# A graph layer on one core: the add of a block's products goes to the head of step 8, and words are unpacked five steps ahead of the turn of their keys

## The chip, the cores and the metric

One core of a Trainium2 chip. The metric is the device time of one launch in microseconds (us), the median of several runs. The profile is of one execution of the same program.

## The reference

One graph layer on 6250 nodes of 64 features and 206,250 edges, sorted by their target node:

```
h   = relu(layernorm(x))
msg = h[src] + edge_feat                  # 206250 x 64
agg = segment_sum(msg, dst, 6250)
out = x + relu(agg @ W1 + b1) @ W2 + b2   # 64 -> 128 -> 64
```

## The kernel before, in words

The sum over edges is split in two. The sum of `h[src]` is made as a product: for each group of three target nodes (a "tile" of at most 127 edges) the kernel counts how often each of the 6272 padded source rows occurs, as a matmul of two one-hot matrices, and multiplies the counts with `h`. The sum of the edge features is made by matmuls of the features with one-hot matrices of the target nodes.

**Blocks and steps.** The work is cut into 23 blocks of 84 tiles (252 nodes), each block into 14 steps of 6 tiles. One loop over all steps `n` writes out the order of instructions on every engine by hand (the scheduler takes them as written); `b` is the block and `s` (0 to 13) the step within it. Each engine takes its own instructions in this order, and waits at an instruction until what it needs is there. The parts of a step, in the order in which the loop calls them:

- `tops` and `before`: lists of small jobs that are hung on single steps (copies of turned keys, unpacking, the checks "over" of L897, the adds of a bias `add_b2`, L1049).
- `count(n)`, on odd steps: 12 matmuls `pc<-hotb` (L962) on TensorE; ScalarE then copies the counts to a ring in SBUF (`ring<-pc`, L971).
- `rows_of_tiles`, on every third step: two VectorE instructions that make `hotb` (L949), the one-hot rows of 18 tiles (three steps), about three steps ahead of the counts that read them.
- `encode`, on every sixth step (n % 6 == 2): three VectorE instructions (L932 twice, L938) that prepare the rows of 36 tiles.
- `products(b - 1, ...)`, at steps 1, 3, 5 and 7: 12, 12, 12 and 13 matmuls `pv<-ring,h` (L981) for the block before.
- `add_products(b - 1)`, at step 8: VectorE adds that block's finished products from PSUM to the sums in SBUF (L1016, in the first four blocks the copy L1014). The block is then `ready`.
- `mlp`, at step 10 (and at step 5 for a few blocks that come late): `ph<-sums,w1s` (L1059) of the ready block on TensorE, relu on ScalarE (L1061); some steps later the second product (`po`, L1067), its add to `x` on VectorE (L1073) and the store.
- `later` and `turns`: jobs that earlier steps have hung on this one. Among them are the sums of edge features. A block has three units of two chunks; VectorE makes a unit's one-hot matrix `hotf` (L496) at steps 3, 6 and 10, and TensorE multiplies it with the features into `bank` (L509) at step 9 (first unit, 48 matmuls) and step 11 (second and third unit, 96 matmuls). `hotf` has two buffers.

`ph`, `po`, `pw`, `pcols` and `over` share one PSUM buffer, one after the other.

**Words and keys.** The positions of a tile's edges come as packed words, 128 tiles at a time and two such lists in one fetch: an indirect DMA `words<-packed` on POOL's queue, which is otherwise full of gathers `pfeat<-table` (rows of `h` for the last 17 groups of edges, eight gathers for a group, summed by L572). `unpack` decodes two lists in four parts on VectorE, one part a step: the fields (L725 to L728), the offsets (L732, L735), the check (L738, L739) and the digits (L743 to L749). At step `n`, the turn of the keys, TensorE transposes them (`pk`, L762). The planner looks for the last step early enough, and prefers step 13 of a block:

```
TURNS = (13, 8, 3)
...
n = min((n for n in range(deadline(c0) + 1 - TURN[-1][0]) if n % STEPS in (TURNS if i > 2 else (4 * i - 2,)) and c1 - R <= encoded(n)),
        key=lambda n: (i > 2 and TURNS.index(n % STEPS), -n))
```

For the pairs i = 4, 6, 8, 10, 12 and 14 this gives step 13 of blocks 4, 7, 10, 13, 16 and 19 (the last pair has one list only). The unpacking begins `ahead` steps before that, and the fetch of the words is put at the head of POOL's list 16 steps before the unpacking. Which gathers POOL gets in a step is decided by an estimated clock and by gates at steps 9 and 11, so the fetch's place moves the gathers around it.

Of the kernel before, what the change touches and what calls it, by code (L numbers as in the profile page):

```python
# [68 lines left out]
SB = 3  # L69
# [3 lines left out]
FRESH = 8  # L73
# [78 lines left out]
def gnn_kernel(ctx: ExitStack, tc: tile.TileContext, x, src_t, dst_t, dst_g, edge, w1, b1, w2, b2, out):  # L152
# [10 lines left out]
    def nodes(b):  # L163
        return start[b + 1] - start[b]
# [4 lines left out]
    def block_of(n):  # L169
        b = min(n // STEPS, NW - 1)  # L170
        return b, n - b * STEPS
# [360 lines left out]
    def at_columns(b, a, z):  # L532
        return [(u, v, c - ring_from(b)) for u, v, c in ring_runs(b, a, z)]
# [174 lines left out]
    def fetch_pair(i0):  # L708
        n = min(2, IC - i0)
        fetch_words(i0, n, P, [first_i[:, i:i + 1] for i in range(i0, i0 + n)])  # L710
# [91 lines left out]
    def unpack_pair(i0):  # L802
        n = min(2, IC - i0)
        return unpack(i0, n, P, nfirst[:, i0:i0 + n], min(P, NWIN - i0 * P) if n == 1 else P)
# [3 lines left out]
    def columns(i):  # L808
        a, z = i * P, min(i * P + P, NWIN)
        mid = min(max(SX, a), z)  # L810
        return [(u - a, v - a, u + o) for u, v, o in ((a, mid, 0), (mid, z, NX)) if u < v]
# [115 lines left out]
    def encode(k):  # L927
        c, n = k * EB % R, min(EB, TILES - k * EB)
        at = work.tile([P, EB, 2, A8], BF16, name="at", bufs=1)
        of = work.tile([P, EB, 2, WE], BF16, name="of", bufs=1)  # L930
        for to, iota_k, m, key in ((at, iota_a, A8, kq[:, 0]), (of, iota_w, WE, kq[:, 1])):
            nc.vector.tensor_tensor(  # L932
                to[:, :n].rearrange("s i k (m o) -> s (i k) m o", o=2),
                iota_k.rearrange("s (m o) -> s m o", o=2).unsqueeze(1).to_broadcast([P, 2 * n, m // 2, 2]),
                key[:, c:c + n].rearrange("s i k o -> s (i k) o").unsqueeze(2).to_broadcast([P, 2 * n, m // 2, 2]),
                op=OP.is_equal)
        pairs_of = of[:, :n].rearrange("s i k (m o) -> s (i k) m o", o=2)
        nc.vector.tensor_tensor(pairs_of, pairs_of, kv[:, c:c + n].rearrange("s i k o -> s (i k) o").unsqueeze(2)  # L938
                                .to_broadcast([P, 2 * n, WE // 2, 2]), op=OP.mult)
        codes[k] = at, of  # L940

    def rows_of_tiles(j):
        if j * HT >= TILES or j in hots:
            return
        at, of = codes[j * HT // EB]
        o, n = j * HT % EB, min(HT, TILES - j * HT)
        hot = hotb[:, j % HOTS]
        for k, c, m in ((0, 0, WS), (1, WS * A8, WL)):
            nc.vector.tensor_tensor(  # L949
                hot[:SLOTS, :n, c:c + m * A8].rearrange("s i (w a) -> s i w a", a=A8),  # L950
                at[:SLOTS, o:o + n, k].unsqueeze(2).to_broadcast([SLOTS, n, m, A8]),
                of[:SLOTS, o:o + n, k, :m].unsqueeze(3).to_broadcast([SLOTS, n, m, A8]), op=OP.mult)
        hots[j] = hot.bitcast(F8)

    def count(n):

        t0 = (n - 1) * ST
        m = min(PAIR, TILES - t0)
        pc = ps.tile([P, 1024], F32, tag="pc", name="pc")
        for j in range(m):  # L960
            hot = hots[(t0 + j) // HT][:, (t0 + j) % HT]
            nc.tensor.matmul(pc[:, j * WPC:j * WPC + HI], hot[:, :P], hot[:, P:P + HI], start=True, stop=True)  # L962
        b, s = block_of(n - 1)
        own = HI - (BY_VECTOR if n == NSTEP - 1 else 0)
        of = pc.bitcast(U8).rearrange("p (m h k) -> p h m k", h=WPC, k=4)
        for u, v, c in ring_runs(b, s * SC, s * SC + m * V):
            to = ring[:, :, c:c + v - u].rearrange("p h (m k) -> p h m k", k=V)
            u, v = u // V - s * ST, v // V - s * ST
            ends = (0, FIRST, own) if b < NW - 1 and s == STEPS - 2 else (0, own)
            for h, z in zip(ends, ends[1:]):  # L970
                nc.scalar.activation(to[:, h:z], of[:, h:z, u:v, :V], AF.Copy)  # L971
            if own < HI:
                nc.vector.tensor_copy(to[:, own:], of[:, own:HI, u:v, :V])

    def products(b, a, z):

        if a == 0:
            pvs[b] = ps.tile([P, 512], F32, tag="pv", name="pv")[:, :columns_of_block(b)]
        c = ring_from(b)
        for h in range(a, z):  # L980
            nc.tensor.matmul(pvs[b], h2[:, h, :], ring[:, h, c:c + columns_of_block(b)], start=(h == 0), stop=(h == HI - 1))  # L981
# [26 lines left out]
    def add_products(b):  # L1008
        pv = pvs.pop(b)
        n = nodes(b)  # L1010
        for a, z, c in at_columns(b, 0, n):
            to = agg[:, start[b] + a:start[b] + z]
            if b <= SB:
                nc.vector.tensor_copy(to, pv[:, c:c + z - a])  # L1014
            else:
                nc.vector.tensor_tensor(to, to, pv[:, c:c + z - a], op=OP.add)  # L1016
        if b == SB:
            for a, z, c in at_columns(b, n, n + NX * V):
                nc.vector.tensor_copy(tail[:, a - n:z - n], pv[:, c:c + z - a])
# [187 lines left out]
    def deadline(c):  # L1207

        return c // EB * EB // ST - EB // ST + AHEAD - 1
# [4 lines left out]
    def encoded(n):  # L1214

        return ((n - AHEAD) * ST // EB + 2) * EB

    def unpack_later(n, f):
        fs = []
        before.setdefault(n, []).append(lambda: fs.extend(f()))  # L1220
        for k in range(4):
            before.setdefault(n + k, []).append(lambda k=k: fs[k]())

    def turn_later(n, i, p, cols):
        for k, f in TURN:
            (turns if f in "kv" else tops).setdefault(n + k, []).append(
                {"k": lambda: turn_keys(i, p), "v": lambda: turn_values(i, p), "0": lambda: key_copies(i, 0, cols),
                 "1": lambda: key_copies(i, 1, cols), "p": lambda: value_powers(i, cols)}[f])

    for i in range(1, IC):  # L1230
        c0, c1 = columns(i)[0][2], columns(i)[-1][2] + columns(i)[-1][1] - columns(i)[-1][0]
        n = min((n for n in range(deadline(c0) + 1 - TURN[-1][0]) if n % STEPS in (TURNS if i > 2 else (4 * i - 2,)) and c1 - R <= encoded(n)),
                key=lambda n: (i > 2 and TURNS.index(n % STEPS), -n))
        if i > 1 and i % 2 == 0:
            ahead = 9 if i > 2 else 4
            before.setdefault(max(n - 16 - ahead, 3), []).append(lambda i=i: i > 2 and queue.insert(
                0, (WORDS_US * 2, lambda: fetch_pair(i))))
            unpack_later(n - ahead, lambda i=i: unpack_pair(i))
        assert n <= (NW - 1) * STEPS + 7
        turn_later(n, i, P, columns(i))  # L1240
# [11 lines left out]
    def clock(n):  # L1252

        return n * HEAD_US if n < STEPS else STEPS * HEAD_US + (n - STEPS) * STEP_US
# [6 lines left out]
    ready = []  # L1261
# [35 lines left out]
    assert len(PART) == FRESH + 1  # L1297
    for n in range(NSTEP):
        b, s = block_of(n)
        for f in tops.get(n, []) + before.get(n, []):  # L1300
            f()
        if n % 2:
            count(n)
        if n % (HT // ST) == 0:
            rows_of_tiles(n // (HT // ST) + 1)
        if n % (EB // ST) == AHEAD and n // (EB // ST) * EB + EB < TILES:
            encode(n // (EB // ST) + 1)
        if b and 1 <= s < FRESH:
            products(b - 1, PART[s], PART[s + 1])
        if b and s == FRESH:  # L1310
            add_products(b - 1)
            if b - 1 > SB:
                ready.append(b - 1)
        if n in SECONDS:
            k = SECONDS.index(n)
            add_seconds(2 * k)
            if 2 * k + 2 >= NX:
                ready[:0] = range(SB + 1)
        if s in LAYERS and ready:
            mlp(ready.pop(0), n, LAYERS[s])  # L1320
        for f in later.pop(n, []) + turns.pop(n, []):
            f()
        pair_ends(n)
        if n >= 3:
            if s in (GROUPS if b < NW - 1 else LAST_GROUPS) and h_next < G and fetched.get(h_next, 1e9) + LAND_US <= clock(n + 2):
                group_hot(h_next)
                at_step(n + 2, features_h, h_next)
                h_next += 1
                add_later(n + 5)
            if n == 3:  # L1330
                pool[0] = clock(n - 1) + OPENING_US
            pool_until(clock(n) + LAND_US)
# [5 lines left out]
    b = NW - 1  # L1338
# [148 lines left out]
```

## Time and profile before

| | |
|---|---|
| median of 3 runs | 392.6 us (389.06 to 393.69) |
| the profiled execution | 391.7 us |
| its span, first to last instruction | 390.0 us |
| mean granted TensorE clock | 0.987 |
| busy: TensorE, VectorE, ScalarE, POOL | 85%, 80%, 84%, 69% |

A row of the timeline gives the start in us, the time taken, the engine (PE is TensorE, DVE VectorE, ACT ScalarE, POOL GpSimd), the line, the instruction with output and inputs, how many are merged (x), and in brackets how long the engine stood idle before it and what ended that. A row of the waits gives who waited for whom: us in total, times, longest.

### The profile page before, as it was taken

What the parts mean: (1) busy time and instruction counts of PE and PEld (TensorE: products, weight loads), DVE (VectorE), ACT (ScalarE), POOL (GpSimd) and SP (SyncE); (2) the same over time, 40 slices, a digit from 0 to 9 for tenths busy, and PEclk for the clock granted to TensorE, in tenths of its full rate; (3) what the DMA queues carried; (4) which work ended last, traced back from release to release, by engine and by line L of the source; (5) the groups of instructions that cost most, each with busy time, mean ns of one, the idle gap of its engine ahead of it and who ended that gap; (6) DMA issues with size and microseconds to landing.
All of it is one profiled execution on the core that took longest, in us unless ns stands there. A gap on an engine that the chain in (4) does not pass through costs nothing.

```text
span 390.0 us, 17219 instructions
## 1 busy us (share of the span) xinstructions
PE 329.7 (85%) x7297; PEld 304.7 (78%) x7298; DVE 312.2 (80%) x814; ACT 326.3 (84%) x376; POOL 270.2 (69%) x206
## 2 busy tenths in 40 slices
PE   2043289989799989889989999899999999999983
PEld 1033278879789979878889999799989989998872
DVE  5758999999988968959799869977998789789320
ACT  6466679999879869989899999999989899999710
POOL 8574588888867867587777788678877787788100
PEclk9999999999989999999999999999999999999988
DMA  7935896969848869759579789868977986798300
GB/s 158 281 100 194 302 306 157 242 145 258 229 102 204 237 165 231 215 117 309 144 207 264 182 206 256 227 165 219 269 195 185 258 246 154 167 279 206 75 15 20
DMA packets 111954, 76.93 MB, mean 197 GB/s; under 512 B 30853, under 2 KB 107773, under 8 KB 111871
## 3 DMA queue, kind: packets, MB, share of 16 engines
q1 hardware_dynamic: 89076, 66.71, 56.8%
q0 software_dynamic: 20560, 8.28, 16.1%
q8 instruction: 59, 0.97, 1.1%
q10 hardware_dynamic: 2235, 0.79, 0.8%
q14 instruction: 24, 0.20, 0.1%
HBM read 71.49 MB, written 4.26 MB: 194 GB/s over the span
## 4 chain that ended last, share of the span: by engine, by line
PE 56%; DVE 9%; ACT 2%; DMA 2%; issue 1%; DVEq 0%; ACTq 0%
PE pv L981 26%; PE pc L962 9%; PE bank L509 8%; PE ph L1059 3%; DVE hotb L949 3%; PE po L1067 2%; PE pv L541 2%; PE bank L572 2%; DMA dstq<-in_dst_g,cols_i 2%; ACT ring L971 1%; PE pk L762 1%; DVE hotf L496 1%; DVE sums L1016 1%; PE pw L769 1%; ACT after L1061 1%
## 5 line engine op out<-in xcount | busy, mean ns | idle before, releaser
L971 ACT ACTIVATE ring<-pc 128x1764 fp32r<-128x1764 uint8 (+2 forms) x183 | 262.3, 1488 | 16.4 <-PE pc L962 13.5
L352 POOL DMA_INDIRECT pfeat<-table,src_p x132 | 222.7, 1687 | 70.3 <-PE bank L509 34.7
L981 PE MATMUL pv<-ring,h 128*128 128x252 f32 x1127 | 156.6, 289 | 1.4 <-ACT ring L971 1.0
L981 PEld LDWEIGHTS pv<-ring,h 128*128 128x128 f32 x1127 | 139.4, 191 | 2.5 <-ACT ring L971 2.0
L949 DVE TENSOR_TENSOR hotb<-at,of 127x576 int32<-127x576 bf16 x216 | 120.5, 600 | 1.6 <-DVE of L938 0.5
L962 PE MATMUL pc<-hotb 128*128 128x49 fp8e5 x1932 | 78.5, 186 | 1.5 <-ACT ring L971 0.7
L962 PEld LDWEIGHTS <-hotb 128*128 128x128 fp8e5 x1932 | 68.0, 98 | 10.8 <-issue 2.2
L509 PE MATMUL bank<-feat,hotf 128*18 128x64 f32 x3288 | 57.6, 222 | 2.2 <-DVE hotf L496 1.2
L509 PEld LDWEIGHTS bank<-feat,hotf 128*18 128x18 f32 x3288 | 48.4, 99 | 5.0 <-DVE hotf L496 1.5
L496 DVE TENSOR_TENSOR hotf<-rel,iota 128x432 f32<-128x432 bf16 x69 | 41.2, 597 | 1.4 <-PE bank L509 1.2
L1016 DVE TENSOR_TENSOR sums<-sums,pv 128x252 f32<-128x252 f32 (+2 forms) x28 | 8.5, 330 | 30.0 <-PE pv L981 30.0
L932 DVE TENSOR_TENSOR at<-iota_a,kq 128x576 bf16<-128x576 bf16 (+1 forms) x54 | 24.4, 451 | 0.2
L352 POOL DMA_INDIRECT words<-packed,first_i x15 | 18.6, 1238 | 7.4 <-issue 4.3
L1059 PE MATMUL ph<-sums,w1s 128*128 128x252 f32 (+2 forms) x50 | 17.1, 425 | 6.8 <-DVE sums L1016 3.9
L1061 ACT ACTIVATE after<-ph,b1s 128x252 f32<-128x252 f32 (+2 forms) x25 | 11.8, 473 | 12.4 <-PE ph L1059 12.4
L938 DVE TENSOR_TENSOR of<-of,kv 128x288 bf16<-128x288 bf16 (+1 forms) x54 | 16.8, 311 | 2.9 <-DVE of L932 0.5
L302 PE MATMUL psrc<-shift,src 128*64 128x128 f32 (+1 forms) x16 | 4.1, 435 | 17.7 <-ACT src L299 17.7
L352 POOL DMA_INDIRECT sums<-in_dst_g,row_i x15 | 15.7, 1048 | 4.6 <-issue 3.7
L782 ACT ACTIVATE kq<-pk 128x512 bf16<-128x512 f32 (+18 forms) x48 | 18.0, 465 | 0.2 <-PE pk L762 0.2
L302 PEld LDWEIGHTS psrc<-shift,src 128*64 128x64 f32 (+1 forms) x16 | 3.1, 244 | 17.7 <-ACT src L299 13.0
L932 DVE TENSOR_TENSOR of<-iota_w,kq 128x288 bf16<-128x288 bf16 (+1 forms) x54 | 16.4, 304 | 0.0
L1067 PE MATMUL po<-w2s,after 128*126 128x64 f32 (+2 forms) x100 | 15.8, 280 | 0.6 <-ACT after L1061 0.6
(187 smaller groups left out, 307.6 us busy)
## 6 DMA issues: line engine op xcount, KB each, us to landing
feat<-in_edge SPq DMA_DIRECT2D x137, 384.0 KB
pfeat<-in_edge SPq DMA_DIRECT2D x16, 256.0 KB
pfeat<-table,src_p POOLq DMA_INDIRECT x132
out_y<-after SPq DMA_DIRECT2D x23, 63.0 KB
xl<-in_x SPq DMA_DIRECT2D x2, 512.0 KB
table<-xl SPq DMA_DIRECT2D x2, 512.0 KB
after<-in_x SPq DMA_DIRECT2D x4, 252.0 KB
table<-xl SPq DMA_DIRECT2D x1, 544.0 KB
```

Of the source, the lines that this page charges most:

```text
L352: ins = nc.gpsimd.indirect_dma_start(out=rows, out_offset=None, in_=source, in_offset=bass.IndirectOffsetOnAxis(ap=index, axis=0), compute ...
L496: nc.vector.tensor_tensor(hot_of[u][:, :n].rearrange("p c j w -> p (c j) w"), rel[:, c:c + n].rearrange("p c q k -> p (c q k)").unsqueeze( ...
L509: ins = nc.tensor.matmul(bank[q * QP:q * QP + WQ, at:at + D], hot_of[u][:, c, j, :], feats[u][c][:, j, :], start=(k == 0), stop=(k == JP - 1))
L782: nc.scalar.activation(kq[:, q, at:at + n].rearrange("s i k o -> s (i k) o"), pk[:, q, a:a + n].rearrange("s i k -> s (i k)").unsqueeze(2) ...
L932: nc.vector.tensor_tensor(to[:, :n].rearrange("s i k (m o) -> s (i k) m o", o=2), iota_k.rearrange("s (m o) -> s m o", o=2).unsqueeze(1).t ...
L938: nc.vector.tensor_tensor(pairs_of, pairs_of, kv[:, c:c + n].rearrange("s i k o -> s (i k) o").unsqueeze(2) .to_broadcast([P, 2 * n, WE // ...
L949: nc.vector.tensor_tensor(hot[:SLOTS, :n, c:c + m * A8].rearrange("s i (w a) -> s i w a", a=A8), at[:SLOTS, o:o + n, k].unsqueeze(2).to_br ...
L962: nc.tensor.matmul(pc[:, j * WPC:j * WPC + HI], hot[:, :P], hot[:, P:P + HI], start=True, stop=True)
L971: nc.scalar.activation(to[:, h:z], of[:, h:z, u:v, :V], AF.Copy)
L981: nc.tensor.matmul(pvs[b], h2[:, h, :], ring[:, h, c:c + columns_of_block(b)], start=(h == 0), stop=(h == HI - 1))
L1059: nc.tensor.matmul(ph[:, :n], w1s, agg[:, start[b]:start[b + 1]], start=True, stop=True)
L1067: nc.tensor.matmul(po[:pairs[b], k, :], hid[:, k:2 * pairs[b]:2], w2s, start=True, stop=True)
```

## The change

Two edits. `add_products` moves from behind the products of step 8 to the head of that step, ahead of `tops`, `before`, `rows_of_tiles` and `encode`. And `ahead` is 5 instead of 9 for the pairs of lists behind the first: the unpacking runs at steps 8 to 11 of the block in whose step 13 the keys are turned, not at 4 to 7, and the fetch of the words moves by the same four steps.

```
@@ the planner of words @@
-            ahead = 9 if i > 2 else 4
+            ahead = 5 if i > 2 else 4
             before.setdefault(max(n - 16 - ahead, 3), []).append(lambda i=i: i > 2 and queue.insert(
                 0, (WORDS_US * 2, lambda: fetch_pair(i))))
             unpack_later(n - ahead, lambda i=i: unpack_pair(i))
@@ the loop over steps @@
     for n in range(NSTEP):
         b, s = block_of(n)
+        if b and s == FRESH:
+            add_products(b - 1)
+            if b - 1 > SB:
+                ready.append(b - 1)
         for f in tops.get(n, []) + before.get(n, []):
             f()
...
         if b and 1 <= s < FRESH:
             products(b - 1, PART[s], PART[s + 1])
-        if b and s == FRESH:
-            add_products(b - 1)
-            if b - 1 > SB:
-                ready.append(b - 1)
```

`FRESH` is 8 and `SB` is 3.

VectorE in block 15, around step 8 (`at`, `of` and L938 are the encode, `sums<-sums,pv` is the add of the products, the pair `hotb` the rows of step 9, `hotf` the third unit's matrix of step 10). Before:

```order
L932 TENSOR_TENSOR at<-iota_a,kq 128x576
L932 TENSOR_TENSOR of<-iota_w,kq 128x288
L938 TENSOR_TENSOR of<-of,kv 128x288
L1016 TENSOR_TENSOR sums<-sums,pv 128x252
L949 TENSOR_TENSOR hotb<-at,of 127x18x32
L949 TENSOR_TENSOR hotb<-at,of 127x18x16
L496 TENSOR_TENSOR hotf<-rel,iota 128x432
```

The same place in the changed kernel:

```order
L1016 TENSOR_TENSOR sums<-sums,pv 128x252
L932 TENSOR_TENSOR at<-iota_a,kq 128x576
L932 TENSOR_TENSOR of<-iota_w,kq 128x288
L938 TENSOR_TENSOR of<-of,kv 128x288
L949 TENSOR_TENSOR hotb<-at,of 127x18x32
L949 TENSOR_TENSOR hotb<-at,of 127x18x16
L496 TENSOR_TENSOR hotf<-rel,iota 128x432
```

The encode has moved from ahead of the add to between the add and `hotf`.

VectorE in block 16, a block with unpacking, from the add at step 8 to `hotf` of step 10. Before, with the last part of the unpacking (`code`) still ahead of it:

```order
L747 TENSOR_SCALAR code<-code 128x512
L749 TENSOR_TENSOR code<-code,near 128x256
L949 TENSOR_TENSOR hotb<-at,of 127x18x32
L949 TENSOR_TENSOR hotb<-at,of 127x18x16
L1016 TENSOR_TENSOR sums<-sums,pv 128x144
L1016 TENSOR_TENSOR sums<-sums,pv 128x108
L949 TENSOR_TENSOR hotb<-at,of 127x18x32
L949 TENSOR_TENSOR hotb<-at,of 127x18x16
L496 TENSOR_TENSOR hotf<-rel,iota 128x432
```

The same place in the changed kernel (fields, offsets and check of the unpacking are L725 to L739):

```order
L1016 TENSOR_TENSOR sums<-sums,pv 128x108
L725 TENSOR_SCALAR code<-words 128x256
L726 TENSOR_SCALAR code<-words 128x256
L728 TENSOR_SCALAR node<-words 128x256
L732 TENSOR_SCALAR near<-node,nfirst 128x128 x2
L735 TENSOR_SCALAR near<-near 128x256
L738 TENSOR_SCALAR near<-near 128x256
L739 TENSOR_SCALAR other,inside<-near 128x2x127
L949 TENSOR_TENSOR hotb<-at,of 127x18x32
L949 TENSOR_TENSOR hotb<-at,of 127x18x16
L496 TENSOR_TENSOR hotf<-rel,iota 128x432
```

Three of the four parts of the unpacking now stand between the add and `hotf`; the fourth follows it.

POOL's queue, from the second fetch on (`pfeat` are the gathers of groups, `words<-packed,first_i` the fetches of blocks 4 and 7's words), with the difference of the two kernels:

```order
 L352 DMA words<-packed,second_i 14x128
-L352 DMA pfeat<-table,src_p 128x64 x15
+L352 DMA pfeat<-table,src_p 128x64 x16
 L352 DMA words<-packed,first_i 128x128 x2
-L352 DMA pfeat<-table,src_p 128x64 x17
+L352 DMA pfeat<-table,src_p 128x64 x18
 L352 DMA words<-packed,first_i 128x128 x2
```

One gather more goes ahead of each of these fetches.

More of the change, by code (lines that the diff above doesn't have):

```diff
@@ L1234, in gnn_kernel @@
         if i > 1 and i % 2 == 0:
-            ahead = 9 if i > 2 else 4
+            ahead = 5 if i > 2 else 4
             before.setdefault(max(n - 16 - ahead, 3), []).append(lambda i=i: i > 2 and queue.insert(
@@ L1299, in gnn_kernel @@
         b, s = block_of(n)
+        if b and s == FRESH:
+            add_products(b - 1)
+            if b - 1 > SB:
+                ready.append(b - 1)
         for f in tops.get(n, []) + before.get(n, []):
@@ L1309, in gnn_kernel @@
             products(b - 1, PART[s], PART[s + 1])
[L1310 to L1313, printed above, removed]
         if n in SECONDS:
```

## The prediction

> **What bounds the kernel now.** I read the page's busy shares first, then the chain that ended last, then the waits, and last the timeline of single blocks.
>
> ```profile
> PE 329.7 (85%) x7297; PEld 304.7 (78%) x7298; DVE 312.2 (80%) x814; ACT 326.3 (84%) x376; POOL 270.2 (69%) x206
> ...
> PE 56%; DVE 9%; ACT 2%; DMA 2%; issue 1%; DVEq 0%; ACTq 0%
> ```
> ```profile
> DVE sums L1016 <- PE pv L981: 30.0, 14, 4.0
> ```
> The busy shares alone would not decide: three engines lie between 80% and 85%. The chain does: 56% of the span is TensorE (PE), 9% VectorE (DVE). And the longest wait of VectorE is for TensorE: 14 times it stands idle ahead of the add of a block's products (L1016), 30.0 us in all. So in most blocks VectorE is early when it reaches the add, and TensorE is the engine whose idle time costs. The question for each moved instruction is then: does it leave a place where VectorE would have waited anyway, and whom does it delay where it goes?
>
> One undisturbed block (15), VectorE's rows, then TensorE's (columns: start us, us taken, instruction, idle before and what ended it):
>
> ```profile
> 270.94 0.42 DVE L1016 TENSOR_TENSOR sums<-sums,pv 128x252 f32<-128x252 f32 x1 [2.28 <-PE pv L981]
> 271.27 1.12 DVE L949 TENSOR_TENSOR hotb<-at,of 127x576 int32<-127x576 bf16 x2
> 272.31 0.60 DVE L496 TENSOR_TENSOR hotf<-rel,iota 128x432 f32<-128x432 bf16 x1
> ...
> 273.98 0.46 DVE L932 TENSOR_TENSOR at<-iota_a,kq 128x576 bf16<-128x576 bf16 x1
> ...
> 274.92 0.55 DVE L519 COPY after<-bank 128x384 f32<-128x384 f32 x1
> ```
> ```profile
> 269.16 1.74 PE L981 MATMUL pv<-ring,h 128*128 128x252 f32 x13
> ...
> 271.94 0.69 PE L1059 MATMUL ph<-sums,w1s 128*128 128x252 f32 x2
> ...
> 272.86 1.54 PE L509 MATMUL bank<-feat,hotf 128*18 128x64 f32 x96
> ```
> The last products end at 269.16 + 1.74 = 270.90; call that moment T. TensorE then runs without a gap; it wants the sum at 271.94 (ph, step 10), and in step 11 it runs 96 chunk matmuls, of which the second half (from 272.86 + 0.77 = 273.63, T + 2.73) reads the hotf that VectorE makes in step 10. That hotf ends at 272.91: **0.72 us ahead of need.** From these rows also come the prices of the moved pieces: a pair of hotb (rows_of_tiles) 272.31 - 271.27 = 1.04, the three instructions of an encode 274.92 - 273.98 = 0.94.
>
> That a late hotf really stops TensorE is seen in block 4, where VectorE does more after the add:
>
> ```profile
> 114.68 0.61 DVE L496 TENSOR_TENSOR hotf<-rel,iota 128x432 f32<-128x432 bf16 x1
> ```
> ```profile
> 115.34 0.86 PE L509 MATMUL bank<-feat,hotf 128*18 128x64 f32 x48 [0.50 <-DVE hotf L496]
> ```
>
> **The change, part by part.** No instruction is added or removed. The sum has four terms.
>
> *1. The add first, plain blocks.* Step 8 falls on an encode in every third block (6, 9, ... 21) and on a pair of hotb in every third (5, 8, ... 20). Before, they ran in the time in which VectorE waited for the products, at no cost; now they stand between the add and hotf. Seven blocks carry nothing else (5, 11, 12, 14, 15, 18, 20), two (17, 21) also an add of the bias L1049 that lay ahead of the add and now lies behind it. First and last of the nine:
>
> ```profile
> 126.75 0.60 DVE L496 TENSOR_TENSOR hotf<-rel,iota 128x432 f32<-128x432 bf16 x1
> ...
> 352.68 0.60 DVE L496 TENSOR_TENSOR hotf<-rel,iota 128x432 f32<-128x432 bf16 x1
> ```
> ```profile
> 127.34 1.54 PE L509 MATMUL bank<-feat,hotf 128*18 128x64 f32 x96
> ...
> 353.23 1.53 PE L509 MATMUL bank<-feat,hotf 128*18 128x64 f32 x96
> ```
> ```profile
> L1049 DVE TENSOR_TENSOR after<-after,b2s 126x512 f32<-126x512 f32 (+2 forms) x7 | 4.4, 627 | 0.0
> ...
> L554 DVE TENSOR_TENSOR sums<-sums,after 128x42 f32 x17 | 3.4, 202 | 4.2 <-ACT after L574 3.1 <-PE ph L1059 0.7
> ```
> Slack from hotf's end to the middle of the 96: 0.76 in block 5, 0.72 in block 21, over the nine 0.35 to 0.83, mean 0.67. Moved work (1.04 or 0.94, mean 0.99) less slack: 0.32 x 9 = 2.9; two L1049 of 0.6: 1.2; in block 12 a 0.2 us sum of a group moves ahead of the add, -0.2. Together **+3.9 us**. Bounds: 0, if the wait is taken up elsewhere, to 9 x 0.99 + 1.2 = 10.1, if none of the slack is there; I take the difference, since both sides are rows of the same blocks.
>
> *2. The add first, blocks 6, 8 and 9.* There an add of an output block (L1073) follows in step 8 and frees the one PSUM buffer that the next instruction needs.
>
> ```profile
> 188.62 0.29 DVE L1073 TENSOR_TENSOR after<-po,after 126x128 f32<-126x128 f32 x1
> ```
> ```profile
> 189.00 0.61 ACT L897 ACTIVATE over<-rel,edge_w 128x411 f32<-128x411 bf16 x1 [0.65 <-DVE after L1073]
> ```
> ```profile
> 189.79 0.69 PE L1059 MATMUL ph<-sums,w1s 128*128 128x252 f32 x2
> ```
> ```profile
> PE ph L1059 <- ACT over L897: 1.5, 2, 1.1
> ...
> PE pcols L425 <- DVE after L1073: 0.4, 1, 0.4
> ```
> In block 9 the chain add, L1073, over, ph has no slack; encode and L1049 now lie ahead of L1073: 0.94 + 0.6 = 1.5. In block 8 (one of the two where ph waits for over already) a hotb pair goes ahead, less the group sum: 0.8. In block 6 the encode goes ahead of L1073, for which TensorE waits already (pcols): 0.9. Together **+3.2 us** (0 to 3.2).
>
> *3. Unpacking at steps 8 to 11, blocks 7, 10, 13, 16, 19.* Its turn of keys is always at step 13, so nine steps ahead was step 4, five ahead is step 8, right behind the add. Block 16 before, and the shorter last list of block 19:
>
> ```profile
> 277.81 0.51 DVE L725 TENSOR_SCALAR code<-words 128x256 int16<-128x256 int16 x1 [0.58 <-PE pw L769]
> ...
> 281.31 0.45 DVE L932 TENSOR_TENSOR at<-iota_a,kq 128x576 bf16<-128x576 bf16 x1
> ...
> 285.45 0.47 DVE L1016 TENSOR_TENSOR sums<-sums,pv 128x144 f32<-128x144 f32 x2
> 285.84 1.12 DVE L949 TENSOR_TENSOR hotb<-at,of 127x576 int32<-127x576 bf16 x2
> ...
> 318.89 0.23 DVE L725 TENSOR_SCALAR code<-words 128x128 int16<-128x128 int16 x1 [0.62 <-PE pw L769]
> ...
> 321.73 0.45 DVE L932 TENSOR_TENSOR at<-iota_a,kq 128x576 bf16<-128x576 bf16 x1
> ```
> ```profile
> 285.98 0.69 PE L1059 MATMUL ph<-sums,w1s 128*128 128x252 f32 x2 [0.76 <-DVE sums L1016]
> ```
> The waits between 125 and 350 us:
> ```profile
> PE ph L1059 <- DVE sums L1016: 3.4, 3, 1.4
> ```
> What it saves: the add comes too late in blocks 10, 13 and 16 (3.4 us), and in block 7 by way of over (the 1.1 above): **-4.5**. What it costs: three quarters of the unpacking stand ahead of hotf, 281.31 - 277.81 less one hotb pair = 2.46. Add 0.39 (285.84 - 285.45) + 2.46 + 1.04 + 0.60 and a 0.05 start: hotf ends at T + 4.54, wanted at T + 2.73: TensorE stands 1.81 in blocks 10 and 16, with L1049 2.41 in block 13, with a narrower L1049 and L1073 some 2.35 in block 7, and 0.66 less (321.73 - 318.89 - 1.04 = 1.80) in block 19: 1.15. That is 9.5; net **+5.0 us**. Bounds: -4.5, if the unpacking hid behind the slack, to +6.5: the last quarter also pushes L519 and L1073, by an estimate from the same durations 0.3 a block.
>
> *4. Block 4.* The moved unpacking delays the hotf of 114.68, for which TensorE waits already, by 2.46. Against it, POOL's queue: the fetch of words moves four steps, and one gather that stood behind it goes ahead.
>
> ```profile
> 96.23 1.56 POOL L352 DMA_INDIRECT words<-packed,first_i  x1 [0.30 <-issue]
> ...
> 99.37 1.92 POOL L352 DMA_INDIRECT pfeat<-table,src_p  x1 [0.30 <-PE bank L509]
> ```
> ```profile
> 102.49 1.64 PE L981 MATMUL pv<-ring,h 128*128 128x252 f32 x12
> ...
> 107.08 0.44 PE L572 MATMUL bank<-after,pfeat 128*64 128x42 f32 x2 [2.00 <-DMA pfeat<-table,src_p]
> ...
> 107.96 2.68 PE L981 MATMUL pv<-ring,h 128*128 128x252 f32 x12
> ...
> 245.71 0.66 PE L1059 MATMUL ph<-sums,w1s 128*128 128x252 f32 x2 [1.43 <-DVE sums L1016]
> ```
> ```profile
> 108.00:109.00 1.00, 1.00 (x9) 1.00 (x6) 0.92 (x4) 1.00 (x2) 1.00 (x1) 0.50 0.87 56
> ...
> 246.00:248.00 2.00, 2.00 (x110) 1.80 (x108) 1.97 (x6) 1.59 (x2) 0.17 (x1) 1.00 1.11 323
> ```
> (In a row of a stretch the last three numbers are granted clock, DMA share, GB/s.) TensorE waits 2.00 us for this very gather (the third group's 24th), issued now at about 96.2 and not 99.4: 3.1 us earlier, the wait is gone. Behind the wait the granted clock was 0.50 and twelve products took 2.68, not 1.64: another 1.04 saved. Net 2.5 - 3.0 = **-0.6 us** (-3 to +2.5). The later words still have a block's time to land; the fetches of dstq keep their places between the gathers, and the two groups that are summed a slot earlier had their gathers moved ahead too: nothing for these.
>
> [...]
>
> By the row at 107.96, the two new stalls over 2 us beside block 4's (7 and 13) and block 4's own may each cost some 1.0 more; behind the 1.43 of block 13 before, the clock stayed at 1.00. A fall by chance is not for the sum; I put 3 us of it into the upper end.
>
> **Sum:** 3.9 + 3.2 + 5.0 - 0.6 = 11.5 us. The profiled execution took 391.7 us (span 390.0, 1.7 around it), 0.9 below the median of the runs shown; on it the sum gives **403.2 us**, 2.9% more.
>
> **Rivals.**
> *The add is what counts (faster).* If the 96 chunk matmuls could wait without loss, or hotf's slack were over 2.5 us, terms 1 and 3's costs vanish, and what stays is -4.5 of ph's waits, -3.0 of the gather, and perhaps term 2's 3.2: 387.4, or 384.2 without it. For it: ph's waits for the sum are the largest between TensorE and VectorE. Against it: the slack is 0.35 to 0.83, and block 4 shows the stop. It would need hotf over 1 us earlier than the rows have it. Chance 5%, of which 2% lie over 2% faster (383.8), where the noise adds to its lower end.
> *Half the costs are taken up.* ScalarE is busy 84%, and where TensorE would next have waited for it a stall costs nothing; with half of terms 1 to 3's stalls (16.6 of stalls and delays, 8.3) hidden, 391.7 + 8.3 - 4.5 - 0.6 = 394.9. Against it: the chain gives ScalarE 2%. Chance 27%, from 392 to 399.
> *The clock falls too:* 406 to 408, by the row of 107.96. Chance 13%.
> *The change doesn't reorder:* the order of instructions is written out and VectorE takes it as written; 1%.
> My forecast, 399 to 406, holds 54%.
>
> **Chances and range.** Two per cent (7.9 us) is about what a measurement of this kernel tells from no change. Slower by more (over 399.6): all of the forecast but its lowest end, and the clock, 0.65. Faster by more: 0.02. Within: the rest, 0.33. The range takes in half-hidden costs and the clock: 395 to 408.
>
> **What would show it.** L1016's waits for pv grow from 30.0 to about 40 us, in nearly every block (VectorE arrives about 1 us earlier, 4 with unpacking); "bank L509 <- hotf" grows from 1.2 to 12 us or more; ph's waits for sums vanish, those for over grow by 2 to 3; the 2.00 us at L572 and the 0.50 clock at 107 vanish. Wrong it would be if the second half of the 96 doesn't wait, or if the time from one add of products to the next stays as it is.

## The result, and the profile after

The changed kernel took 406.9 us (median of 6 runs, 406.27 to 409.92) beside 391.0 us for the kernel before in the same place: 1.0457 of before, 95% interval 1.041 to 1.0505. The profiled run took 407.4 us, its span was 405.6 us. Slower was forecast, by 2.9%, at 403.2 us; it is slower by 4.6%.

The page of the changed kernel, the busy shares and the chain:

```profile
PE 332.5 (82%) x7297; PEld 305.3 (75%) x7298; DVE 311.3 (77%) x814; ACT 326.8 (81%) x376; POOL 274.0 (68%) x206
...
PE 53%; DVE 25%; issue 3%; ACT 3%; DVEq 0%; ACTq 0%
```

VectorE works no longer than before (311.3 against 312.2 us), but its share of the chain went from 9% to 25%: in more places TensorE now waits for it. The waits of the changed kernel say where (engine and line that wait, what for, us in all, times, longest):

```profile
DVE sums L1016 <- PE pv L981: 45.1, 19, 4.0
...
PE bank L509 <- DVE hotf L496: 14.2, 18, 2.2
...
PE ph L1059 <- ACT over L897: 3.7, 3, 1.6
...
PE pcols L425 <- DVE after L1073: 1.3, 1, 1.3
...
PE ph L1059 <- DVE sums L1016: 0.5, 1, 0.5
```

TensorE's waits for the third `hotf` and for the sums in the kernel before:

```profile
PE ph L1059 <- DVE sums L1016: 3.9, 4, 1.4
...
PE bank L509 <- DVE hotf L496: 1.2, 2, 0.7
```

The first row is VectorE's: it reaches the add earlier and stands there 45.1 us, not 30.0. What it would have done in those 15 us now comes behind the add, most of it ahead of `hotf`, and TensorE waits 14.2 us at L509, not 1.2. The wait for the checks grew from 1.5 to 3.7 us, that of pcols from 0.4 to 1.3; that of ph for the sums fell from 3.9 to 0.5.

Block 16 in a second profile of the changed kernel (span 403.0 us, below), VectorE's rows and then TensorE's:

```profile
292.36 0.48 DVE L1016 TENSOR_TENSOR sums<-sums,pv 128x144 f32<-128x144 f32 x2 [2.38 <-PE pv L981]
292.76 0.29 DVE L725 TENSOR_SCALAR code<-words 128x256 int16<-128x256 int16 x1
...
295.15 1.12 DVE L949 TENSOR_TENSOR hotb<-at,of 127x576 int32<-127x576 bf16 x2
296.19 0.60 DVE L496 TENSOR_TENSOR hotf<-rel,iota 128x432 f32<-128x432 bf16 x1
```
```profile
294.29 0.86 PE L509 MATMUL bank<-feat,hotf 128*18 128x64 f32 x48
296.84 0.87 PE L509 MATMUL bank<-feat,hotf 128*18 128x64 f32 x48 [1.69 <-DVE hotf L496]
```

From the start of the add to the end of `hotf` it is 296.19 + 0.60 - 292.36 = 4.43 us, and the 96 chunk matmuls stop in the middle for 1.69 us. So 4.43 - 1.69 = 2.74 us of that list are free: the prediction had 2.73 from rows of block 15.

**Two kinds of place.** The experiments were run in six sets. In two of them the kernel before takes 387 to 397 us, as in its first runs; in the other four it takes 411 to 419 us; below these are the places of the second kind. Times and ratios are compared within a set only. The times given are medians of all runs, while the ratios leave out runs that took over 1.5% longer than the fastest run of the same kernel. Profiles are compared across sets too, between the two sets of the first kind (with the second profile of the kernel before) unless it is said otherwise.

### The profile page after: what moved, and what is told of

Same layout as the page of the kernel before. It is cut to its first block, busy times and chain, and to the rows that moved or that the text cites. A ratio compares the mean times of both kernels' runs of the same rounds, so it can differ in the third digit from the quotient of the medians.

```text
span 405.6 us, 17234 instructions
## 1 busy us (share of the span) xinstructions
PE 332.5 (82%) x7297; PEld 305.3 (75%) x7298; DVE 311.3 (77%) x814; ACT 326.8 (81%) x376; POOL 274.0 (68%) x206
## 4 chain that ended last, share of the span: by engine, by line
PE 53%; DVE 25%; issue 3%; ACT 3%; DVEq 0%; ACTq 0%
PE pv L981 30%; PE pc L962 8%; DVE hotb L949 7%; PE bank L509 4%; PE pv L541 3%; DVE hotf L496 3%; PE bank L572 2%; DVE at L932 2%; ACT ring L971 2%; PE po L1067 2%; DVE of L938 2%; DVE sums L1016 1%; PE ph L1059 1%; DVE of L932 1%; DVE near L732 1%
## 5 line engine op out<-in xcount | busy, mean ns | idle before, releaser
L352 POOL DMA_INDIRECT pfeat<-table,src_p x132 | 227.7, 1725 | 79.3 <-PE bank L509 43.1
L509 PE MATMUL bank<-feat,hotf 128*18 128x64 f32 x3288 | 60.5, 224 | 14.2 <-DVE hotf L496 14.2
L509 PEld LDWEIGHTS bank<-feat,hotf 128*18 128x18 f32 x3288 | 48.9, 100 | 19.5 <-DVE hotf L496 17.4
L1016 DVE TENSOR_TENSOR sums<-sums,pv 128x252 f32<-128x252 f32 (+2 forms) x28 | 8.5, 331 | 45.1 <-PE pv L981 45.1
L352 POOL DMA_INDIRECT words<-packed,first_i x15 | 16.7, 1116 | 9.0 <-DVE first_i L382 3.4
L352 POOL DMA_INDIRECT sums<-in_dst_g,row_i x15 | 16.8, 1118 | 4.6 <-issue 4.3
L938 DVE TENSOR_TENSOR of<-of,kv 128x288 bf16<-128x288 bf16 (+1 forms) x54 | 16.7, 308 | 3.1 <-DVE of L932 0.5
```

What stands on the lines that cost most here:

```text
L352: ins = nc.gpsimd.indirect_dma_start(out=rows, out_offset=None, in_=source, in_offset=bass.IndirectOffsetOnAxis(ap=index, axis=0), compute ...
L509: ins = nc.tensor.matmul(bank[q * QP:q * QP + WQ, at:at + D], hot_of[u][:, c, j, :], feats[u][c][:, j, :], start=(k == 0), stop=(k == JP - 1))
```

## The experiments

**The kernel before and after again, side by side.**

> The kernel before once more, unchanged, for its profile on the chip of these runs: on the chip of the first four runs it took 412.6 us, and their traces show 26 to 32 stops of TensorE within a group of counts (L962) that the profile puts down to nothing (12 us in all), where the first trace of before has one. If chips differ in this, the new trace has either about 1 us of such stops and 388 to 394 us, or about 12 us and 410 to 416 us.

> The changed kernel, unchanged, on the same chip. Theory (its cost is made by waits on VectorE, and stops of TensorE's own take some of VectorE's lateness up): on a chip without those stops 1.04 to 1.05 of before, with 13 to 16 us of waits of L509 on hotf; on a chip with them a smaller ratio, 1.02 to 1.04, with under 8 us of such waits. Rival (the two edits each cost what they cost in the first runs, 2.4% and 1.9%, whatever the chip): 1.04 to 1.05 on either, with waits of L509 that don't matter.

The kernel before: 390.5 us in its profiled run (span 388.8). The changed kernel: 406.1 us (404.71 to 409.73), 1.0454 of before (1.0245 to 1.0663), profiled run 404.7 us (span 403.0), with 13.9 us of waits for `hotf`, as the theory had it for a place without TensorE's own stops (last section). With this pair the loss can be put down to blocks: the time from the first L541 of a block (step 3) to that of the next, in the profiles, changed kernel less before, in us. The last two columns belong to the experiments that follow and are taken against the second profile of before.

| blocks (step of the prediction) | forecast | first pair | second pair | add first alone | unpacking alone |
|---|---|---|---|---|---|
| 1 to 3 (in no step) | 0 | +1.0 | +0.8 | +1.1 | +0.1 |
| 5, 11, 12, 14, 15, 17, 18, 20, 21 (1) | +3.9 | +6.0 | +4.1 | +4.5 | -1.5 |
| 6, 8, 9 (2) | +3.2 | +4.0 | +4.0 | +4.7 | -0.9 |
| 7, 10, 13, 16, 19 (3) | +5.0 | +5.3 | +5.5 | -0.6 | +0.6 |
| 4 (4) | -0.6 | -1.4 | +0.1 | -0.3 | -0.2 |
| ahead of block 1's, and from block 22's on | 0 | +0.7 | -0.4 | -1.7 | -1.4 |
| span | +11.5 | +15.6 | +14.2 | +7.7 | -3.3 |

**Each edit alone.** The add first, unpacking nine steps ahead as before:

```diff
-            ahead = 5 if i > 2 else 4
+            ahead = 9 if i > 2 else 4
```

> The add alone stands first in step 8; the words are unpacked nine steps ahead, as before. Theory (late hotf: VectorE waits at the add for the last of pv, everything that it makes in steps 8 to 10 comes after that wait, and TensorE stops at L509 for the third hotf): the two terms of the prediction that belong to this edit, 3.9 + 3.2, and some 2 us of lower clock that the sum left out, so 398 to 401 us; waits of L509 on hotf of 6 to 9 us in all, spread over all blocks from 5 on. Rival (the move of the unpacking is the main part, the add costs little): 392 to 395 us, L509's waits under 3 us.

> The add alone stands first in step 8, as in the first run, now to be read beside a profile of before from a chip without TensorE's own stops (on such a chip; if this one has them, the run says no more than the first). Theory (late hotf): waits of L509 on hotf of 0.3 to 0.8 us in each block from 1 on, 6 to 9 us in all, and waits of ph for the checks of 2 to 4 us, less the 3.5 us of waits for the sums that go: 1.015 to 1.025 of before. Rival (this edit costs little without the other): under 1.01.

The unpacking five steps ahead, the add in its old place (diff against before):

```diff
-            ahead = 9 if i > 2 else 4
+            ahead = 5 if i > 2 else 4
```

> The words are unpacked five steps ahead (steps 8 to 11), the add stands in its old place in step 8, behind the first piece of unpacking. Theory: the unpacking in steps 8 to 11 delays the third hotf in six blocks only, about as much as the unpacking in steps 4 to 7 stopped TensorE before (5.0 against 4.5), and block 4 gains 3.0 us from the fetch that no longer stands ahead of the gather: 389 to 392 us. Rival (the move of the unpacking is the main part of the 16 us): 397 to 403 us.

> The unpacking alone, five steps ahead, as in the second run, again for a chip without TensorE's own stops. Theory: six blocks lose about 1 us each to a later hotf, the stalls that the unpacking in steps 4 to 7 made (3.5 us) go, and block 4 gains 0 to 3 us, so 0.99 to 1.005 of before. Rival (by what the first chip showed, 1.019): the sums that come behind the unpacking or its hotf are later than the working has them, 1.015 to 1.025, with over 8 us of waits of L509 on hotf.

The first run of each fell into a place of the second kind: 1.0236 (1.0179 to 1.0292) and 1.0191 (1.0149 to 1.0233) of before. In a place of the first kind the add first gave 399.1 us, 1.0238 (1.0157 to 1.0319), and the unpacking alone 389.1 us, 0.9989 (0.9952 to 1.0026). Both came out as the theory had them there, except that with the add first ph still waits 2.7 us for the sums, where none was expected; the 1.0191 of the first place did not, and without a profile of before from that place I cannot say why. TensorE's waits, first with the add first alone, then with the unpacking alone:

```profile
PE bank L509 <- DVE hotf L496: 6.2, 12, 1.1
...
PE ph L1059 <- ACT over L897: 3.9, 3, 1.6
PE ph L1059 <- DVE sums L1016: 2.7, 4, 0.8
```
```profile
PE bank L509 <- DVE hotf L496: 4.9, 7, 1.9
...
PE ph L1059 <- DVE sums L1016: 0.5, 1, 0.5
```

The table's last columns show what the edits do apart. The add first makes all of steps 1 and 2, to within 0.7 us of the second pair, and costs nothing in the five blocks that unpack. The unpacking alone costs those blocks 0.6. Together they cost them 5.5: about 5.5 us more than the sum of the two. The waits for `hotf` in these blocks are 0.3, 2.3 and 6.6 us. That is most of the step from 1.0238 and 0.9989 to 1.045.

The reason is in the lists. With the unpacking alone one part of it, the fields, stays ahead of the add, in VectorE's wait. Block 16 there:

```profile
280.87 0.48 DVE L1016 TENSOR_TENSOR sums<-sums,pv 128x144 f32<-128x144 f32 x2 [1.63 <-PE pv L981]
...
283.68 0.60 DVE L496 TENSOR_TENSOR hotf<-rel,iota 128x432 f32<-128x432 bf16 x1
```
```profile
284.34 0.87 PE L509 MATMUL bank<-feat,hotf 128*18 128x64 f32 x48 [0.68 <-DVE hotf L496]
```

The list takes 283.68 + 0.60 - 280.87 = 3.41 us, and TensorE waits 0.68: again 2.73 are free. In that block the wait of ph for the sums (0.48 in the second profile of before) is gone, so little is lost. With the add first and the old unpacking only a pair of `hotb` lies between, and block 16 does not wait for `hotf`. The 2.73 us of slack can be used once.

**Does the length of the list set the wait?** The changed kernel with the unpacking seven steps ahead:

```diff
-            ahead = 5 if i > 2 else 4
+            ahead = 7 if i > 2 else 4
```

> The changed kernel with the words unpacked seven steps ahead, so that two of the four pieces stand before the add (in VectorE's wait for pv), and two behind it: 0.9 us ahead of the third hotf and not 2.5. Theory (the two edits meet in the blocks that unpack: what stands between the add and the hotf adds up there, and each alone is covered by 0.7 us of slack or by a wait that it removes): the five blocks 7, 10, 13, 16, 19 lose about 1.6 us less each, down to what the add alone leaves there, so 7 of the 16 us less nearly 5: 1.025 to 1.035 of before, with waits of L509 on hotf of 7 to 9 us. Rival (it is the place of the fetches and of the turns behind them that costs, not the length of the list): within 2 us of the changed kernel, 1.04 to 1.05.

> The unpacking seven steps ahead with the add first, again, for a chip without TensorE's own stops (the chip before had them, 413.6 us for the kernel before). Theory as there: 1.025 to 1.035 of before, the waits of L509 on hotf in blocks 7, 10, 13, 16 and 19 under 0.5 us each (1.1 to 1.7 in the changed kernel). Rival: 1.04 to 1.05, those waits as in the changed kernel.

> The unpacking seven steps ahead with the add first, beside the changed kernel in the same place. Two runs of it in a place with TensorE's own stops gave 1.037 and 1.044, with waits of L509 on hotf of 4.6 us in blocks 7, 10, 13, 16 and 19 together. Theory (length of the list): less than the changed kernel by 2 us or more, and those waits less by 1.5 us or more, here or there. Rival (fetches and turns): as the changed kernel within 1 us.

> The changed kernel once more, for the comparison with the run beside it. Without TensorE's own stops as before, 1.04 to 1.05 and 6 to 7 us of waits of L509 on hotf in the five blocks that unpack; with them 1.04 to 1.05 too if the waits on VectorE don't depend on the stops.

All four runs fell into places of the second kind. Unpacking seven steps ahead: 1.0373 (1.0304 to 1.0442), 1.0442 (1.0362 to 1.0522) and 1.0486 (1.0415 to 1.0557). The changed kernel beside the last took 429.0, 430.2, 439.4 and 439.7 us, the kernel before 414.3; by the two shorter runs it is about 1.037, without an interval. So no gain is seen, and the theory's time failed. The rival's "as the changed kernel" did not hold to 1 us either: seven steps took some 6 us longer than those two runs, and in the profiles over 4 us of this lie in blocks 10, 13 and 16, where the clock fell to 0.50 (last section). My expectation miscounted the list. The parts now fall on steps 6 to 9, and `hotf` is made late in step 10, so the check and the whole last part stand ahead of it: not 0.9 us but nearly as much as before. Block 16 with seven steps (VectorE, TensorE), then the changed kernel beside it:

```profile
317.64 0.48 DVE L1016 TENSOR_TENSOR sums<-sums,pv 128x144 f32<-128x144 f32 x2 [1.70 <-PE pv L981]
...
321.14 0.60 DVE L496 TENSOR_TENSOR hotf<-rel,iota 128x432 f32<-128x432 bf16 x1
```
```profile
321.80 0.86 PE L509 MATMUL bank<-feat,hotf 128*18 128x64 f32 x48 [0.99 <-DVE hotf L496]
```
```profile
313.11 0.48 DVE L1016 TENSOR_TENSOR sums<-sums,pv 128x144 f32<-128x144 f32 x2 [2.41 <-PE pv L981]
...
316.88 0.60 DVE L496 TENSOR_TENSOR hotf<-rel,iota 128x432 f32<-128x432 bf16 x1
```
```profile
317.53 0.68 PE L509 MATMUL bank<-feat,hotf 128*18 128x64 f32 x33 [1.27 <-DVE hotf L496]
```

Lists of 4.10 and 4.37 us, waits of 0.99 and 1.27: both leave 3.1 us free (2.73 elsewhere; in these places TensorE also stops by itself on the way). The same reading for blocks 10, 13 and 19 gives, list and wait, seven steps against five: 4.10 and 0.97 against 4.38 and 1.24; 4.75 and 1.72 against 4.56 and 1.37; 3.64 and 0.50 against 3.69 and 0.56. In all eight, list less wait lies between 3.03 and 3.19 us, and VectorE stands idle nowhere within a list. In the second profile of the changed kernel, from a place of the first kind, list less wait is 2.72 to 2.74 us in ten blocks (5, 11, 12, 14 to 16 and 18 to 21). So the wait follows the length of the list one for one, longer and shorter; that the fetches or turns are to blame is not needed. A list truly half as long was not run.

The place takes up a part of the loss. TensorE's waits for `hotf` in the changed kernel are 7.9 us here, against 13.9 in the place of the first kind, with 1.037 and 1.045 of before:

```profile
PE bank L509 <- DVE hotf L496: 7.9, 10, 1.7
```

For a place with TensorE's own stops under 8 us and 1.02 to 1.04 had been expected.

**Taking `hotf` away from behind the add.** First by making it in step 7, with the first unit's chunk sums moved to step 5 so that its buffer is free (after, and before as control):

```diff
-CHUNKS = ((9, 9), (11, 11), (11, 11))
+CHUNKS = ((5, 5), (11, 11), (11, 11))
-HOT_AT = (3, 6, 10)
+HOT_AT = (3, 6, 7)
```

> The changed kernel with the third hotf made in step 7, ahead of the add, and so that a buffer is free for it, the first unit's chunk sums in step 5 and not 9. Theory: the waits of L509 on hotf (14.2 us in the changed kernel) go to under 2 us, what is left are the mlp's waits in blocks 6, 8 and 9 with their clock fall (4 us) and the gain of 3 us in block 4: 391 to 396 us. Rival (VectorE is late with everything, so the next thing that it makes, hotb for the counts or the outputs' sums, stops TensorE in place of hotf): 400 to 407 us, with waits of L962 or L769 on VectorE of over 8 us.

> The control: the kernel before with the same move of the third hotf to step 7 and the first chunk sums to step 5. Theory: its L509 waits for hotf only 1.2 us in all, so nothing more than that is to be had: 389 to 392 us. Rival (the move of the hotf and of the chunk sums is worth something by itself, so that the third run says little of the add): under 387 or over 395 us.

Both missed: 1.0657 (1.06 to 1.0714) and, the control, 1.0539 (1.0465 to 1.0613), in a place of the second kind. The control's waits:

```profile
DVE hotf L496 <- PE bank L509: 15.6, 7, 3.4
...
DVE sums L1016 <- PE pv L981: 10.5, 8, 2.6
...
PE ph L1059 <- DVE sums L1016: 7.3, 10, 2.0
```

VectorE, which runs ahead of TensorE, now has to wait for the chunk sums of step 5 before it can make the third `hotf` in the freed buffer (15.6 us, and 15.4 in the changed kernel's run), loses its lead (at the add it waits 10.5 us and not 30.0), and is late with the sums. These two say nothing of the change; they priced a buffer. So the third `hotf` got a place of its own, in memory that is free from block 7 on, and the chunk sums stayed:

```diff
+        hot_of[u] = third if units[u][0] >= 7 and units[u][3] == 2 else work.tile(...)
+            at_step(n + (... 7 if b >= 7 and at_h == 10 else at_h), chunk_hot, u)
```

> The changed kernel with a place of its own for the third hotf from block 7 on, so that it is made at the end of step 7, ahead of the add, while VectorE would wait for pv anyway; chunk sums and all else stay. Theory: the waits of L509 on hotf in blocks 7 to 21 (9.5 us in the changed kernel's second profile) go, blocks up to 6 keep theirs: 7 to 10 us less than the changed kernel, 1.02 to 1.025 of before. Rival (VectorE's lateness in steps 8 to 12 moves to the next thing that it makes, hotb of the counts): within 3 us of the changed kernel, with waits of L962 on hotb of over 5 us.

> The control: the kernel before with the same third hotf in step 7 from block 7 on. Theory: its L509 waits 1.2 us for hotf in all, and before block 7, so nothing is to be had: 0.995 to 1.005 of before. Rival (an earlier hotf is worth something by itself): under 0.99.

> The unpacking five steps ahead, the add in its old place, and from block 7 on the third hotf in a place of its own in step 7. Theory: the waits on hotf that the unpacking alone left in blocks 10 to 19 (2.0 us) go, nothing else is late: 0.985 to 0.997 of before, the fastest so far. Rival (as in the control, the earlier hotf pushes the add of products back by its 0.6 us, and ph waits for the sums): 1.000 to 1.010, with waits of ph for sums of over 2 us.

> The unpacking alone with the third hotf in step 7, again, for a chip without TensorE's own stops. Theory: 0.985 to 0.997 of before. Rival, which the run on the chip with stops speaks for (1.010): 1.000 to 1.012, the add pushed back by the hotf ahead of it.

With it the changed kernel took 400.7 us, 1.0263 (1.0142 to 1.0384). Its profile's span is 397.7 us, against 403.0 without it: by the spans 5.3 us are back, where 7 to 10 were expected. By the ratios of the two sets it would be some 7 us, with intervals too wide to decide. The waits for `hotf` in blocks 7 to 21 are gone, but most of what they cost in the blocks that unpack comes back a little later:

```profile
PE pw L769 <- DVE after L1073: 5.0, 5, 1.5
...
PE bank L509 <- DVE hotf L496: 4.1, 5, 2.2
```

The 5.0 us are waits, in the block after an unpacking one, for the output add that the whole list has pushed back (0.7 us in the changed kernel). By blocks, the nine of step 1 fall from +4.1 to +1.0, the five of step 3 only from +5.5 to +4.3. So theory and rival each hold in a part: `hotf` is the place where plain blocks lose, and only the first of several in the blocks that unpack.

The control was not neutral: the kernel before with the third `hotf` in step 7 took 1.0076 (1.0033 to 1.0119). In block 16 there:

```profile
286.73 0.60 DVE L496 TENSOR_TENSOR after<-rel,iota 128x432 f32<-128x432 bf16 x1
287.24 0.47 DVE L1016 TENSOR_TENSOR sums<-sums,pv 128x144 f32<-128x144 f32 x2
```
```profile
287.77 0.69 PE L1059 MATMUL ph<-sums,w1s 128*128 128x252 f32 x2 [1.15 <-DVE sums L1016]
```

VectorE is late there already, so 0.60 us of `hotf` ahead of the add is 0.67 us more wait for the sums (0.48 before). And the unpacking alone with the third `hotf` gave 1.0101 (1.007 to 1.0131) and 1.0082 (1.005 to 1.0114), both in places of the second kind. These times are the rival's, but its mechanism is not seen: ph waits only 0.5 us for the sums there, where over 2 had been expected, so the cause of this 1% stays open. No version was found that is shown to beat the kernel before.

**Step 2's output adds.** The changed kernel with the outputs of the early layers a step earlier, so that L1073 goes ahead of the add:

```diff
-LAYERS = {10: 3, 5: 2}
+LAYERS = {10: 3, 5: 1}
```

> The changed kernel with the outputs of the early layers (hidden in step 5) made in step 6 and added in step 7, ahead of the add of products, and not in steps 7 and 8. Theory: the waits of the checks, pcols and ph in blocks 6, 8 and 9 go (3.2 us of the prediction's sum and 1.2 us of lower clock in block 6), the rest stays: 3 to 5 us less than the changed kernel, 1.03 to 1.04 of before. Rival (those waits only hide the lateness of hotf that comes behind them): within 1 us of the changed kernel.

409.0 us, 1.0479 (1.0282 to 1.0676), beside 406.1 for the changed kernel in this set: nothing won, as the rival had it, though not within its 1 us. The waits for the checks are gone, and others stand in their place. Block 7:

```profile
158.86 0.68 PE L1067 MATMUL po<-w2s,after 128*126 128x64 f32 x4 [1.66 <-ACT after L1061]
...
166.00 0.87 PE L509 MATMUL bank<-feat,hotf 128*18 128x64 f32 x48 [1.82 <-DVE hotf L496]
```

The product now waits for ScalarE, and the wait for `hotf` that the wait for the checks had covered (0.44 in the changed kernel) is 1.82.

**Step 4's fetch.** The kernel before with only the fetch of the words later:

```diff
-            before.setdefault(max(n - 16 - ahead, 3), []).append(...)
+            before.setdefault(max(n - (21 if i > 2 else 20), 3), []).append(...)
```

> The kernel before with only the fetch of the words issued four steps later (21 steps ahead of the turn of their keys, not 25); unpacking and add as before. Theory: gather 24 goes ahead of the words, so the 2.0 us wait of L572 in block 4 and the fall of the clock behind it go: 2 to 4 us less than before, 0.990 to 0.995. Rival (the words, now 12 steps ahead of their unpacking, arrive late or push other gathers later): 1.00 to 1.01, with waits of L725 on the words of over 2 us.

397.3 us, 1.0114 (0.9706 to 1.0521): the time says nothing. The waits say more: L572's for the gather is gone (TensorE is busy in all 3.00 us from 104.0 to 107.0), but VectorE now waits for the words in block 4,

```profile
107.57 0.29 DVE L725 TENSOR_SCALAR code<-words 128x256 int16<-128x256 int16 x1 [4.35 <-DMA words<-packed,first_i]
```

and TensorE behind it: it is busy for 0.56 of the 3.00 us from 107.0 on, and for 0.14 of the 3.00 us from 112.5 on. Twelve steps from fetch to unpacking are too few there; the changed kernel, like the kernel before, leaves sixteen. So the later fetch can only be had with the later unpacking.

## Why the prediction was wrong in size, and what of it was right

- **What failed** is the sum, "3.9 + 3.2 + 5.0 - 0.6 = 11.5 us". The pairs of profiles have 15.6 and 14.2. As a ratio, 1.0457 (1.041 to 1.0505) lies beyond the range, whose upper end is 408 beside 391.7, or 1.042. Three things had no term. Blocks 1 to 3 cost +1.0 and +0.8: in block 3 TensorE waits 0.75 us for `hotf`, where it had not waited, and in block 2 for a pair of `hotb` (0.29) and for the ring (0.38). Falls of the clock went only into the upper end, and one makes most of block 6's excess of 1.3: in the first pair, at a clock of 0.50, it is 3.87 us from ph to the counts behind the chunk sums, and 2.36 before. Behind the waits that were counted stand further ones: L907's for VectorE's L904 (`needed`) in block 21 went from 0.33 to 0.90, and L769's for L1073 behind the blocks that unpack, in sum, from none to 0.7. And two savings were counted that did not come, or not in both pairs: 1.1 in block 7 and 1.0 of clock in block 4.
- **The mechanism** was right: who waits first, for what, and in which blocks from 4 on. All the signs came: waits at L1016 from 30.0 to 45.1 (about 40 forecast), L509's for `hotf` from 1.2 to 14.2 (12 or more), ph's for sums from 3.9 to 0.5, those for the checks from 1.5 to 3.7; L572's 2.00 us and the clock of 0.50 at 107 us are gone (it is 1.00 there).
- **Step 1** (+3.9) measured +6.0 and +4.1, and +4.5 with the add first alone. Stops of TensorE that wait for nothing in the profile blur this: 0.82 us in block 18 of the changed kernel's first profile, 0.59 and 0.86 in block 18 of the two profiles of before, and 0.29 in block 15 of the second. Without them the two pairs have 5.8 and 5.3, so the near hit of +4.1 is luck. The waits for `hotf` in the nine blocks, 3.8 in both, are what was forecast; the wait for L904 in block 21 and one of 0.27 for `hotb` in block 17 come on top.
- **Step 2** (+3.2) measured +4.0, and of it block 6 2.2 where 0.9 was forecast. Its wait for L1073 grew by 0.9 as worked out; what was left out is the clock behind it (last section).
- **Step 3** (+5.0) measured +5.3 and +5.5, from smaller parts, so the agreement of the difference is in part luck. The waits for `hotf` in the five blocks add up to 6.6, not 9.5. Blocks 10, 16 and 19 have 1.60, 1.69 and 1.13 (1.81, 1.81 and 1.15 forecast), block 13 1.73 and not 2.41, because its bias add of 0.68 makes the list only 0.24 longer than block 16's (4.67 against 4.43; L732 behind it takes 0.47 and not 0.70), and block 7 0.44 and not 2.35, because it waits for the checks first. That wait for the checks, 1.07 before, was to go and is still 1.00, so about 3 of the 4.5 us came back.
- **Step 4** (-0.6) measured -1.4 against the first profile of before and +0.1 against the second, where the wait for the gather is 1.9 and the clock stayed at 1.00. Of the 3.0 us counted as saved, the 1.0 of clock is thus in one profile of two. The wait for `hotf` grew by 1.7, not 2.46.
- **The rivals.** "Half the costs are taken up" fell: the waits of TensorE from 60 us on add up to about 17 us in the second profile of before and 29 in that of the changed kernel, 12 of the 14.2 us. "The clock falls too" (406 to 408) is where the median of 406.9 lies, with a kernel before that took 391.0 in that place; but the clock fell in block 6 (to 0.50), and not in blocks 4, 7 and 13 (1.00), where this rival had put it.

## What to carry to other kernels

Before an instruction is moved from ahead of a waiting one to behind it, measure the slack of the next thing that the waiting engine owes the bound engine: here 2.73 us from the add to the end of `hotf`, and every 0.1 us of list beyond it was 0.1 us of wait where TensorE waited for nothing else on the way. Two moves that draw on the same slack must be summed before they are compared with it: alone they cost 2.4% and nothing, together 4.5%. And taking away the wait that shows shows the next one: an earlier `hotf` gave back 5.3 of the 14.2 us of span, because the output add had been pushed back by the same list.

## What the hardware showed that I had not expected

**The clock falls in one run and not in another.** In block 6 of the changed kernel two waits lie close together, and behind them the granted clock is 0.50 (the last three numbers: clock, DMA share, GB/s); the kernel before has 1.00 there, behind waits of 0.38 and 1.29 us:

```profile
140.97 0.82 PE L425 MATMUL pcols<-ones,quarters 1*128 1x1 f32 x6 [1.30 <-DVE after L1073]
...
144.01 0.94 PE L1059 MATMUL ph<-sums,w1s 128*128 128x252 f32 x2 [1.02 <-DVE cols L432]
```
```profile
144.50:147.50 3.00, 3.00 (x96) 2.69 (x97) 1.38 (x5) 2.08 (x2) 1.64 (x2) 0.50 1.04 325
```
```profile
142.50:145.50 3.00, 3.00 (x132) 2.86 (x127) 2.03 (x7) 2.79 (x4) 1.54 (x1) 1.00 1.09 308
```

This was so in both profiles of the changed kernel and with the add first alone (0.50 from 144.5 to 147.0 us in all three). Elsewhere the same waits had it once and not another time. Two runs of one program, seven steps ahead, from two sets on different chips, block 13:

```profile
274.36 0.86 PE L509 MATMUL bank<-feat,hotf 128*18 128x64 f32 x48 [1.72 <-DVE hotf L496]
```
```profile
276.50:279.50 3.00, 3.00 (x26) 3.00 (x25) 2.52 (x6) 2.82 (x5) 2.43 (x2) 0.50 1.13 313
```
```profile
273.23 0.86 PE L509 MATMUL bank<-feat,hotf 128*18 128x64 f32 x48 [1.71 <-DVE hotf L496]
```
```profile
274.00:277.00 3.00, 2.45 (x44) 2.24 (x37) 2.89 (x7) 1.52 (x2) 2.69 (x2) 1.00 1.05 322
```

The first run's clock fell to 0.50 in blocks 10, 13 and 16 (block 13 took 17.5 us from L541 to L541, the second run's 16.0), and its span is 435.1 against 429.5 us. In block 4 it was the other way: there the second run's clock stayed low for longer (0.50 from 122.5 to 129.0 us, in the first run from 123.0 to 126.0; the block took 19.4 us against 17.2). Whether chance or the place decides is not shown, nor what sets a fall off: waits of 1.30 and 1.02 us with work between them came ahead of one in block 6, and in block 13 the clock fell behind a wait of 1.72 us and stayed at 1.00 behind one of 1.71.

**TensorE stops by itself in some places.** In the sets in which the kernel before takes 411 to 419 us, TensorE stops within groups of counts for nothing that the profile shows, 8.7 to 13.6 us in six profiles of these sets. The changed kernel in such a place, and then its second profile, from a place of the first kind:

```profile
PE pc L962 <- issue: 12.7, 32, 0.6
```
```profile
PE pc L962 <- issue: 0.3, 1, 0.3
```

The spans are 428.5 and 403.0 us, so the extra 12 us of such stops are about half of the difference. One set of the first kind and two of the second ran on a chip of the same number; what sets the stops, and where the rest goes, stays open.
